# A graph network on one core: one tile of every second block taken from a table in SBUF instead of gathered

## The chip, the core and the metric

The kernel runs on one core of a Trainium2 chip. The metric is the device time of one execution in microseconds: the median of ten runs of the kernel before is 3889.19 us (3887.39 to 3890.49). The engines are TensorE (PE), VectorE (DVE), ScalarE (ACT), GpSimd (POOL) and SyncE (SP). Here GpSimd does little but issue gathers (indirect DMAs), and SyncE issues nearly all other DMAs.

## The reference

A graph of 6250 nodes with 128 features and 200,000 edges, sorted by their target node, goes through two layers. Both start from h = relu(layernorm(x)) and add their result to x. Cut to what matters:

```python
# layer 0, graph attention: 8 heads of 16
z  = h @ W;  el, er = <z, attn_l>, <z, attn_r>          # per node and head
e  = leaky_relu(el[src] + er[dst], 0.2)
a  = exp(e - segment_max(e, dst)[dst])
x += segment_sum(z[src] * a, dst) / segment_sum(a, dst) + bias
# layer 1, tensor product: s, v = parts of h, times W_up
w0..w3 = silu(silu(edge_attr_8 @ A1 + b1) @ A2 + b2) @ A3
mji = (s[src], v[src]) combined with edge_attr_4 and w0..w3   # 256 per edge
x += (segment_sum(mji, dst) / 10) @ W_out
```

Each layer so needs, for every edge, the row of a node table at src: 136 floats (z and el) in layer 0, 128 in layer 1.

## The kernel before

The edges are cut into tiles of 128, and 16 tiles make a block: NB = 98 blocks, the last one cut in two, so NG = 99 groups. Because the edges are sorted, a block's targets lie in a window of 128 nodes, and two blocks close one tile of nodes (NX = 50 tiles).

The first stage computes the table t0 (z and el by node) and writes it to DRAM. It also keeps er of each node as three bf16 parts (er3), whose sum is nearly the fp32 value.

Layer 0 is one loop over groups, `for g in range(NG - 3)` (line 1363). A step g works on several blocks at once: the logits and maxima of block g, the weights and sums of block g - 1 (called b4), the target side of block g + 1 (n1), the 0/1 matrices of block g + 2 (n2), and, every second step, the node stage of a finished tile of nodes. All this is written out by hand, and the order binds TensorE, DVE, ACT and SyncE (`tc.manual_schedule(engines=in_order)`): each runs its instructions in the order of the text. GpSimd has only gathers. The parts that matter here:
- `take_rows(g + 3)` has GpSimd gather the rows of block g + 3, one indirect DMA per tile (`gather`, line 833). The rows go to one of five buffers (`z_pool`), beside `z_first` for block 0, so block 6 needs the buffer of block 1, which is free after `sums` of that block in step 2.
- Of every third block (`by_row`: 3, 6, ... 93) the last tile is not gathered. `rows_by_row` has SyncE fetch its 128 rows one by one, each with its own DMA (line 1078), some blocks ahead. `rows_until` says how far:

```python
while rows_until.n < (block + 3) * P / 12 and next(rows, 0) is None:
    rows_until.n += 1          # one step is four rows
```

  It stands twice at the head of each step, `rows_until(rows, g + 0.5)` and `rows_until(rows, g + 1)`, with the DMAs of the nodes between them (`node_out`, `node_rows`).
- `ends_of` compares each edge's target with the 128 nodes of the window (`one_hot`, line 1097, on DVE): s, edges by nodes. `sums` (line 1234) multiplies s with the weighted rows, fp32, two records per product.
- `turned` (lines 1151 and 1153) transposes s on TensorE, four at a time, and ACT casts the result to bf16: d, nodes by edges. `er_of` (line 1162) multiplies d with the three parts of er.
- `logits`, `maxima`, `neighbours`, `weights`, `weighted` make the softmax weights; the node stage is `node_x` to `node_out`. x of all nodes stays in SBUF (`x_all`).

The bank p_n of PSUM holds a copy of iota, the er of the block (`er_p`), and the node stage's products.

Layer 1 gathers from t1 in the same way, with `by_row` too, and adds its result to x_all. Its first 24 tiles are gathered from t1z, a copy whose last three tiles of nodes are zero, while layer 0 ends.

Of the kernel before, what the change touches and what calls it, by code (L numbers as in the profile page):

```python
# [18 lines left out]
P = 128  # L19
H = 8  # L20
# [721 lines left out]
def tile_even_edges(  # L742
# [88 lines left out]
    def gather(to, table, tiles, width, first=0):  # L831
        for k, t in enumerate(tiles, first):
            nc.gpsimd.indirect_dma_start(  # L833
                out=to[:, k, :width], out_offset=None, in_=table,
                in_offset=bass.IndirectOffsetOnAxis(ap=src_col[:, t : t + 1], axis=0))
        return to
# [128 lines left out]
def even_edges(tc, v):  # L965
# [7 lines left out]
    with ExitStack() as ctx:  # L973
        const = ctx.enter_context(tc.tile_pool(name="fconst", bufs=1))
        z_pool = ctx.enter_context(tc.tile_pool(name="fz", bufs=5))
        s_pool = ctx.enter_context(tc.tile_pool(name="fs", bufs=16))
# [18 lines left out]
        x_all = const.tile([P, NX, P], F32, name="fx_all")  # L995
# [8 lines left out]
        a3p = const.tile([P, 2, P], F32, name="fa3p")  # L1004
        nc.sync.dma_start(a3p, v["a3p"])
# [4 lines left out]
        wout = const.tile([P, 2, P], F32, name="fwout")  # L1010
        nc.sync.dma_start(wout, v["wout"])
        dloc = const.tile([P, NB * KB], F32, name="fdloc")
        identb = l0c.tile([P, P], BF, name="fidentb")
        nc.vector.tensor_copy(identb, ident)
# [8 lines left out]
        with tc.tile_pool(name="fbuild", bufs=1) as build:  # L1023
            d_c = build.tile([P, TU], I32, name="fd_c")
            nc.sync.dma_start(d_c, dstc)
            d_i = build.tile([P, TG, P], I32, name="fd_i")
            nc.sync.dma_start(d_i, tiles_of(dstt, P))
            q_i = build.tile([P, TG, P], I32, name="fq_i")
            nc.sync.dma_start(q_i, tiles_of(dstt, P - 1))
            nxt_i = build.tile([P, TG], I32, name="fnxt")  # L1030
            nc.sync.dma_start(nxt_i, tiles_of(dstt, 2 * P)[:, :, 0])
            off = build.tile([P, TU], F32, name="foffs")
            nc.sync.dma_start(off, nums[:, :TU])
            nc.vector.tensor_sub(dloc[:, :TU], d_c, off)


            eq = build.tile([P, TG, MC], F32, name="feq")
            nc.vector.tensor_tensor(eq[:, :, :P], d_i, q_i, OP.is_equal)
            nc.vector.memset(eq[:, :, 0:1], 0.0)
            nc.vector.memset(eq[:, :, P : P + 1], 0.0)  # L1040
            nc.vector.tensor_tensor(eq[:, :, P + 1 : 2 * P + 1], d_i,
                                    nxt_i.unsqueeze(2).to_broadcast([P, TG, P]), OP.is_equal)
            nc.vector.tensor_tensor(eq[:, :, 2 * P + 1 :], d_i,
                                    q_i[:, :, 0:1].to_broadcast([P, TG, P]), OP.is_equal)
            for g in range(TG):
                nc.scalar.activation(masks[:, g, :], eq[:, g, :], AF.Copy, bias=-BIG, scale=BIG)

            zeros = build.tile([P, NL, P], F32, name="fzeros")
            nc.vector.memset(zeros, 0.0)
            nc.sync.dma_start(t1z[LATE * P - W0 :].rearrange("(j p) f -> p j f", p=P), zeros)  # L1050
# [5 lines left out]
        with tc.tile_pool(name="fat_ps", bufs=1, space=PSUM) as at_ps:  # L1056
            col = l0c.tile([P, P], F32, name="fcol")
            n = NB - 1
            nc.vector.tensor_copy(col[:, :n], v["src_col"][:, KB - 1 : n * KB : KB])
            p_c = at_ps.tile([P, P], F32, name="p_c")  # L1060
            nc.tensor.transpose(p_c[:n], col[:, :n], ident)
            for i, w in enumerate((ZW, P)):
                nc.vector.tensor_scalar(at[i][:n], p_c[:n], float(4 * w), None, op0=OP.mult)
# [53 lines left out]

        in_order = {mybir.EngineType.PE, mybir.EngineType.DVE, mybir.EngineType.Activation,
                    mybir.EngineType.SP}
        with tc.manual_schedule(engines=in_order), \  # L1120
                tc.tile_pool(name="l0", bufs=2) as l0, \
                tc.tile_pool(name="l0n", bufs=2) as l0n, \
                tc.tile_pool(name="l0_ps", bufs=1, space=PSUM) as l0_ps:
# [3 lines left out]
            p_n = l0_ps.tile([P, 512], F32, name="p_n")  # L1127
            er_p, iota_p = p_n[:, P : 2 * P].rearrange("p (t h) -> p t h", h=H), p_n[:, 3 * P :]
            nc.scalar.copy(iota_p, iota)

# [14 lines left out]

            def turned(c, q):
                if 4 * q < c["kt"]:
                    m = min(4, c["kt"] - 4 * q)
                    p_d = l0_ps.tile([P, 4, P], F32, name="p_d", bufs=2)
                    for k in range(m):  # L1150
                        nc.tensor.transpose(p_d[:, k, :], c["s"][q][:, k, :], ident)  # L1151
                    d = c["d", q] = l0.tile([P, 4, P], BF, name="d", bufs=4)
                    nc.scalar.copy(d[:, :m], p_d[:, :m])  # L1153
# [17 lines left out]
            def logits(c, bank="pe"):  # L1171
                kt = c["kt"]
                kr = kt * H
                e_s = l0.tile([P, KB, H], F32, name="e_s")
                pe = c["pe"] = p_n if bank == "p_n" else l0_ps.tile([P, 512], F32, name=bank, bufs=2)
                nc.vector.tensor_add(e_s[:, :kt], c["z"][:, :kt, F:], c["er"][:, :kt])  # L1176
                nc.vector.scalar_tensor_tensor(e_s[:, :kt], e_s[:, :kt], 0.2, e_s[:, :kt],  # L1177
                                               op0=OP.mult, op1=OP.max)
                nc.tensor.transpose(pe[:kr, :P], e_s[:, :kt].rearrange("p t h -> p (t h)"), ident)  # L1179
# [57 lines left out]

            def node_rows(i, n):
                nc.sync.dma_start(x_all[:, i : i + n, :],
                                  xp[i * P : (i + n) * P].rearrange("(j p) f -> p j f", p=P))  # L1240

            def with_bias(i, n):
                x_i = x_all[:, i : i + n, :]
                nc.vector.tensor_add(x_i, x_i, bias_b[:, None, :].to_broadcast([P, n, F]))

            def node_x(u):
                i, n, agg = u["i"], u["n"], u["agg"]
                x_i = x_all[:, i : i + n, :]
                if n == 1:
                    with_bias(i, n)  # L1250
                rd = l0n.tile([P, 2, H], F32, name="rd")[:, :n]
                nc.vector.tensor_scalar(rd, agg[:, :n, F:ZW], 1e-9, None, op0=OP.max)
                nc.vector.reciprocal(rd, rd)
                sums_ = agg[:, :n, :F]
                heads = sums_.rearrange("p j (h d) -> p j h d", d=D)
                nc.vector.tensor_mul(heads, heads, rd.unsqueeze(3).to_broadcast([P, n, H, D]))
                nc.vector.tensor_add(x_i, x_i, sums_)
                u["mv"] = moments(l0n, x_i, n, f"n{n}")
# [4 lines left out]
            def node_h(u):  # L1263
                i, n = u["i"], u["n"]
                rs, mr = normal(l0n, u["mv"], u["rs"], n, f"n{n}")
                xn = u["xn"] = l0n.tile([P, 2, P], F32, name="xn")
                nc.scalar.activation(xn[:, 0, :], x_all[:, i, :], AF.Identity, bias=mr[:, 0, :],
                                     scale=rs[:, 0, :])
                if n == 2:
                    nc.vector.tensor_scalar(xn[:, 1, :], x_all[:, i + 1, :], u["mv"][:, 1, 0:1],  # L1270
                                            rs[:, 1, :], op0=OP.subtract, op1=OP.mult)

            def node_t(u):
                n = u["n"]
                u["p_n"] = p_n.rearrange("p (j f) -> p j f", f=P)
                for j in range(n):
                    nc.tensor.transpose(u["p_n"][:, j, :], u["xn"][:, j, :], ident)
                h_t = u["h_t"] = l0n.tile([P, 2, P], F32, name="h_t")
                nc.scalar.activation(h_t[:, :n], u["p_n"][:, :n], AF.Relu)
# [11 lines left out]
            def node_out(u):  # L1291
                i, n, sv = u["i"], u["n"], u["sv"]
                first = i * P - W0
                for table in (t1, t1z) if i < LATE else (t1,):
                    if i == 0:
                        nc.sync.dma_start(table[: P - W0, :], sv[W0:, 0, :])
                    else:
                        nc.sync.dma_start(
                            table[first : first + n * P].rearrange("(j p) f -> p j f", p=P), sv)

# [12 lines left out]
            def take_rows(g):  # L1313
                if 0 < g < NG:
                    c = cs[g]
                    t = c["b"] * KB + c["o"]
                    c["z"] = gathered(t0, range(t, t + c["kt"] - (c["b"] in by_row)), ZW)
# [28 lines left out]
            for g in range(1, 3):  # L1346
                take_rows(g)
            masks_of(cs[0])
# [14 lines left out]
            for g in range(NG - 3):  # L1363
# [12 lines left out]
                logits(c)  # L1376
                ends_of(n2, 0)
# [3 lines left out]
                maxima(c)  # L1381
                ends_of(n2, 1)
# [5 lines left out]
                er_of(n1, 0)  # L1388
                if b4:
                    weights(b4)  # L1390
                for n in nodes:
# [3 lines left out]
                if b4:  # L1395
                    bank_of(b4)
                    weighted(b4, 0)
                turned(n1, 3)
                er_of(n1, 2)
                if b4:  # L1400
                    weighted(b4, 8)
                for n in nodes:
# [4 lines left out]
                if b4:  # L1407
                    sums(b4, 0)
                for n in nodes:
# [7 lines left out]
                if b4:  # L1417
                    sums(b4, 8)
                if g == NG - 4:
# [68 lines left out]
        with tc.manual_schedule(engines=in_order), \  # L1488
                tc.tile_pool(name="l1", bufs=3) as l1, \
                tc.tile_pool(name="l1n", bufs=2) as l1n, \  # L1490
                tc.tile_pool(name="l1_ps", bufs=2, space=PSUM) as l1_ps:

# [79 lines left out]

            def node1(i, agg):
                x_i = x_all[:, i, :]
# [10 lines left out]
            def node_out1(i):  # L1585
                x_i = x_all[:, i, :]
                if i == 0:
                    nc.sync.dma_start(out[: P - W0, :], x_all[W0:, 0, :])
# [54 lines left out]
            rows, rows_until.n, late = rows_by_row(1, t1, P), 0, []  # L1643
# [13 lines left out]
            for i, u in enumerate(us):  # L1657
                b, k0, m = u["b"], u["k0"], u["m"]
                if k0 == 0:
                    take_rows(b + 2)  # L1660
                    filled(1, b, blk[b]["z"], P)
                    edge_rows(b + 2)
                if k0 == 4:
# [43 lines left out]
            x_i = x_all[:, NX - 2 :, :]  # L1707
# [140 lines left out]
```

## Time and profile before

| | |
|---|---|
| median of ten runs | 3889.19 us |
| the profiled execution | 3889.12 us, its span 3887.3 us |
| mean granted clock of TensorE | 0.802 |
| busy in the span: PE, DVE, ACT, POOL | 73%, 57%, 36%, 75% |
| gathers, all but 32 in one group | 3024, mean 945 ns |
| rows fetched singly by SyncE | 2 x 3968 |
| layer 0, 165 to 1955 us: granted clock | 0.64 |
| layer 1, 2000 to 3867 us: granted clock | 0.97 |

The profile is of one execution. "Busy" counts the time of an engine's instructions, without waits and without the issue of DMAs, so SyncE has no busy share; its instructions are read from the timeline. A group of instructions is shown as line, engine, operation, written tile <- read tiles, count, then busy time, mean ns of one, and the idle time of the engine just before them with what ended it. Times in the timeline are microseconds from the start of the span.

### The profile page before, as it was taken

The numbers are of one execution on the slowest core, as the hardware profiler recorded it, in microseconds if no ns is written. First come the engines' busy times: TensorE is split into PE (matmuls) and PEld (weight loads), VectorE is DVE, ScalarE is ACT, GpSimd is POOL, SyncE is SP. The second block draws the span as 40 slices with busy tenths as digits, with TensorE's granted clock in tenths as the row PEclk, the third lists the DMA queues.
The fourth block names the chain that finished last, engine by engine and source line by source line (L and its number), as shares of the span: only waits on it lengthen the run. The fifth ranks groups of instructions, "written<-read, shape, count | busy, mean of one in ns | idle before, by whom it ended". The sixth has DMA issues, their size and how long they took to land. (4 is left out here: it accounts for less than half of the span.)

```text
span 3887.3 us, 62701 instructions
## 1 busy us (share of the span) xinstructions
PE 2852.6 (73%) x14785; PEld 2405.2 (62%) x14785; DVE 2225.6 (57%) x5408; ACT 1396.7 (36%) x3612; POOL 2912.7 (75%) x3096
## 2 busy tenths in 40 slices
PE   3766666666666666666678888888888777778877
PEld 3656656656666556666666666666766566656665
DVE  5544444444444444444457777677766666666666
ACT  3323232323222323232324444444444444444443
POOL 6777777777777777777777777777777777777776
PEclk6666666666666666666679999999999999999999
DMA  6222222222222222222222222222222222222222
GB/s 180 59 64 64 62 64 64 64 62 64 62 64 62 64 62 64 62 63 62 62 60 61 61 61 62 62 62 62 62 61 61 63 62 61 62 61 63 61 61 50
DMA packets 195262, 252.65 MB, mean 65 GB/s; under 512 B 78656, under 2 KB 145088, under 8 KB 194880
## 3 DMA queue, kind: packets, MB, share of 16 engines
q0 software_dynamic: 98048, 207.27, 22.5%
q1 hardware_dynamic: 96544, 41.19, 4.0%
q8 instruction: 120, 1.97, 0.2%
q14 instruction: 262, 2.15, 0.2%
q10 hardware_dynamic: 288, 0.07, 0.0%
HBM read 234.73 MB, written 13.25 MB: 64 GB/s over the span
## 5 line engine op out<-in xcount | busy, mean ns | idle before, releaser
L833 POOL DMA_INDIRECT g<-ft,fsrc x3024 | 2856.4, 945 | 922.3 <-issue 854.6
L1570 PE MATMUL p_u<-mj,s 128*128 128x256 f32 x3126 | 791.0, 397 | 211.5 <-DVE mj L1562 209.8
L1570 PEld LDWEIGHTS p_u<-mj,s 128*128 128x128 f32 x3126 | 589.3, 196 | 378.3 <-DVE mj L1562 302.9
L1234 PE MATMUL p_u<-g,s 128*128 128x136 f32 x3062 | 597.6, 376 | 0.4 <-DVE g L1229 0.4
L1234 PEld LDWEIGHTS p_u<-g,s 128*128 128x128 f32 x3062 | 571.8, 279 | 0.5 <-DVE g L1229 0.4
L1537 ACT ACTIVATE p_w<-p_w,yb 128x64 f32<-128x64 f32 x1563 | 450.7, 288 | 122.2 <-PE p_w L1533 76.4
L1553 DVE TENSOR_TENSOR vy<-g,p_i 128x384 f32<-128x384 f32 x387 | 213.4, 552 | 355.7 <-DMA g<-ft,fsrc 245.3
L1533 PE MATMUL p_w<-fa3p,h 128*128 128x256 f32 x1564 | 412.7, 387 | 0.0
L1151 PE MATMUL p_d<-fident,s 128*128 128x128 f32 x1563 | 384.9, 412 | 0.0
L1533 PEld LDWEIGHTS p_w<-fa3p,h 128*128 128x128 f32 x1564 | 290.2, 196 | 118.7 <-issue 53.1
L1176 DVE TENSOR_TENSOR e_s<-g,p_n 128x128 f32<-128x128 f32 x96 | 27.5, 287 | 578.8 <-DMA g<-ft,fsrc 558.0
L1518 ACT ACTIVATE h<-p_h,fb 128x512 f32<-128x512 f32 x196 | 134.7, 687 | 576.9 <-PE p_h L1516 576.9
L1151 PEld LDWEIGHTS p_d<-fident,s 128*128 128x128 f32 x1563 | 313.1, 226 | 37.3 <-issue 26.0
L1144 ACT COPY mk<-p_m 128x385 f32<-128x385 f32 (+1 forms) x99 | 47.6, 481 | 782.5 <-PE p_m L1141 782.5
L1229 DVE TENSOR_TENSOR g<-g,pe 128x1024 f32<-128x1024 f32 x193 | 225.6, 1209 | 129.1 <-ACT g L1220 121.1
L1153 ACT CAST d<-p_d 128x512 bf16<-128x512 f32 x391 | 228.5, 585 | 192.2 <-PE p_d L1151 141.2
L1179 PE MATMUL pe<-fident,e_s 128*128 128x128 f32 x98 | 39.3, 401 | 326.6 <-DVE e_s L1177 326.6
L1097 DVE TENSOR_TENSOR s<-p_i,fdloc 128x512 f32<-128x512 f32 x391 | 268.7, 687 | 3.8 <-ACT p_i L1512 3.8
L1097 DVE TENSOR_TENSOR s<-p_n,fdloc 128x512 f32<-128x512 f32 x391 | 266.4, 683 | 6.0 <-ACT sv L1289 2.8
L1516 PE MATMUL p_h<-ft,fa1p 128*128 128x128 f32 x1568 | 217.9, 284 | 65.9 <-DMA ft<-in_e_f_dram 65.8
L1516 PEld LDWEIGHTS p_h<-ft,fa1p 128*128 128x128 f32 x1568 | 211.4, 198 | 86.5 <-issue 67.3
L1523 ACT ACTIVATE h<-p_h,fb 128x512 f32<-128x512 f32 x196 | 134.7, 687 | 306.5 <-PE p_h L1520 306.5
(202 smaller groups left out, 3355.4 us busy)
## 6 DMA issues: line engine op xcount, KB each, us to landing
r<-ft SPq DMA_DIRECT2D x3968, 0.5 KB
r<-ft SPq DMA_DIRECT2D x3968, 0.5 KB
g<-ft,fsrc POOLq DMA_INDIRECT x3024
ft<-in_e_f_dram SPq DMA_DIRECT2D x98, 64.0 KB
yb<-in_e_y_dram SPq DMA_DIRECT2D x98, 32.0 KB
fx_all<-in_e_xp_dram SPq DMA_DIRECT2D x48, 64.0 KB
out_dram<-fx_all SPq DMA_DIRECT2D x47, 64.0 KB
ft<-sv SPq DMA_DIRECT2D x46, 64.0 KB
```

What stands on the lines that cost most here:

```text
L833: nc.gpsimd.indirect_dma_start(out=to[:, k, :width], out_offset=None, in_=table, in_offset=bass.IndirectOffsetOnAxis(ap=src_col[:, t : t + ...
L1097: nc.vector.tensor_tensor(s[:, :m], iota[:, None, :].to_broadcast([P, m, P]), dloc[:, t : t + m].unsqueeze(2).to_broadcast([P, m, P]), OP. ...
L1151: nc.tensor.transpose(p_d[:, k, :], c["s"][q][:, k, :], ident)
L1153: nc.scalar.copy(d[:, :m], p_d[:, :m])
L1229: nc.vector.tensor_mul(zh, zh, p_a[:, k0 : k0 + m].unsqueeze(3).to_broadcast([P, m, H, D]))
L1234: nc.tensor.matmul(c["p_u"][:, :ZW], c["s"][k // 4][:, k % 4, :], c["z"][:, k, :], start=c["o"] + k == 0, stop=c["o"] + k == KT[c["b"]] - 1)
L1516: nc.tensor.matmul(p_h[:, q, :], a1p[:, q0 + q, :], c["ft"], start=True, stop=True)
L1518: nc.scalar.activation(c["h1"], p_h, AF.Silu, bias=b1)
L1533: nc.tensor.matmul(w[:, k : k + n].rearrange("p k a u -> p (k a u)"), c["h2"][q // 4][:, q % 4, :], a3p[:, :n].rearrange("p k f -> p (k f) ...
L1537: nc.scalar.activation(w[:, k, ::2, :], w[:, k, ::2, :], AF.Copy, scale=c["yb"][:, k0 + k, 0:1])
L1553: nc.vector.tensor_mul(vy, v_n, y_p)
L1570: nc.tensor.matmul(blk[b]["p_u"][:, :MW], u["s"][:, k, :], u["mj"][:, k, :], start=k0 + k == 0, stop=k0 + k == KT[b] - 1)
```

## The change

In layer 0, of every second block (`dense`: 7, 9, ... 93, 44 blocks) the tile before the last (`KD` = 14) is not gathered any more. Instead:
- t0 is read back into SBUF in layer 0's first four steps (`split`), two tiles of 128 nodes at a time, and cut into three bf16 parts: `t0s`.
- `spread` has TensorE lay out the tile's sources along the free axis, the same in each partition; `ends_to` has DVE compare them with the nodes of each of NR = 17 tiles: 0/1 matrices, nodes by edges, kept in the space of `z_first`.
- `rows_of` multiplies each of the 17 with three table tiles at once (i, i + 17, i + 34: up to 408 columns), for the three parts, 51 products into one bank. Each edge so gets three candidate rows, and `taken` picks the right one on DVE with the 0/1 weights `part`.

The 0/1 matrix d is not transposed any more: the targets (`d_b`) are written to DRAM at the start (`ends`), SyncE loads those of a block into all partitions (`ends_row`, one 512 KB load per block), and DVE compares them with the node number. x is no longer kept in SBUF: layer 0 loads it by tile, as before, stores it to DRAM (`x1`), and layer 1 loads it again. iota, er and the new columns move to a bank of their own (`held`), the node stage gets p_n for itself. The order of the steps around this stays. The diff, cut to its core:

```diff
+            d_b = build.tile([P, TG, P], BF, name="fd_b")
+            off_t = build.tile([P, TG], F32, name="foff_t")
+            nc.sync.dma_start(off_t, nums[:, NB * KB : NB * KB + TG])
+            nc.vector.tensor_sub(d_b, d_i, off_t.unsqueeze(2).to_broadcast([P, TG, P]))
+            nc.sync.dma_start(ends.rearrange("g t e -> t g e"), d_b)
...
+            def split(i, n):
+                zr = l0.tile([P, 2, ZW], F32, name="zr")[:, :n]
...
+                    nc.sync.dma_start(zr, rest.rearrange("(j p) f -> p j f", p=P))
+                r = l0.tile([P, 2, ZW], F32, name="zr2", bufs=1)[:, :n]
+                nc.scalar.copy(t0s[:, 0, i : i + n, :], zr)
+                nc.vector.tensor_sub(r, zr, t0s[:, 0, i : i + n, :])
+                nc.scalar.copy(t0s[:, 1, i : i + n, :], r)
+                nc.vector.tensor_sub(t0s[:, 2, i : i + n, :], r, t0s[:, 1, i : i + n, :])
+            def spread(c):
+                nc.tensor.matmul(at_p, key[:, b : b + 1].to_broadcast([P, P]), ident, ...)
+            def ends_to(c, h):
+                n = half if h == 0 else NR - half
...
+                nc.vector.tensor_tensor(
+                    oh[:, :n], at_p.unsqueeze(1).to_broadcast([P, n, P]),
+                    place[:, h * half : h * half + n].unsqueeze(2).to_broadcast([P, n, P]), OP.is_equal)
+            def rows_of(c, k0, n):
...
+                    for s in range(3):
+                        nc.tensor.matmul(c["p_x"][:, :m, :], c["oh", k // half][:, k % half, :],
+                                         t0s[:, s, i::NR, :], start=k == 0 and s == 0, ...)
+            def taken(c):
+                nc.vector.tensor_scalar(z, c["p_x"][:, 0, :], part[:, b, 0:1], None, op0=OP.mult)
+                for r in (1, 2):
+                    nc.vector.scalar_tensor_tensor(z, c["p_x"][:, r, :], part[:, b, r : r + 1], z, ...)
+            def ends_row(b):
+                    to = ends_row.tiles[b] = l0.tile([P, KB, P], BF, name="er_d", bufs=2)
+                    nc.sync.dma_start(to, ends[g : g + 1, j * KB : (j + 1) * KB, :].to_broadcast([P, KB, P]))
             def turned(c, q):
-                    for k in range(m):
-                        nc.tensor.transpose(p_d[:, k, :], c["s"][q][:, k, :], ident)
-                    nc.scalar.copy(d[:, :m], p_d[:, :m])
+                    nc.vector.tensor_tensor(d[:, :m], ends_row.tiles[c["b"]][:, k0 : k0 + m],
+                                            node_p.unsqueeze(2).to_broadcast([P, m, P]), OP.is_equal)
...
+                nc.sync.dma_start(x1[i : i + n].rearrange("j p f -> p j f"), x_of.pop(i))   # node_out
...
+            for b in range(2):
+                ends_row(b)                       # ahead of the first rows
             for g in range(NG - 3):
...
                 logits(c)
+                ends_row(g + 2)
+                to, was = n2["b"] in dense, n1["b"] in dense
+                if to:
+                    spread(n2)
                 ends_of(n2, 0)
...                                               # masks_of, turned, maxima
+                if to:
+                    ends_to(n2, 0)
+                if was:
+                    rows_of(n1, half, 4)
...                                               # neighbours, turned, er_of
+                if was:
+                    rows_of(n1, half + 4, NR)
...                                               # weights, then: if was: taken(n1)
                     weighted(b4, 0)
+                if to:
+                    ends_to(n2, 1)
...                                               # turned(n1, 3), er_of, weighted(b4, 8)
+                if to:
+                    rows_of(n2, 0, 3)
...                                               # er_of, sums(b4, 0)
+                if to:
+                    rows_of(n2, 3, 3)
...                                               # nodes, er_sum, sums(b4, 8)
+                if to:
+                    rows_of(n2, 6, half - 6)
+                for i in range(g * 14, min(g * 14 + 14, NX), 2):
+                    split(i, min(2, NX - i))
```

In layer 1 x is loaded two blocks at a time by `node_rows1`, at the head of each even block, behind that block's `edge_rows`; the loads of a3p and wout move from the start of the kernel to the start of layer 1.

## The prediction

> **What bounds the kernel now.** I read the costliest groups first, then the busy times by stage.
>
> ```profile
> L833 POOL DMA_INDIRECT g<-ft,fsrc x3024 | 2856.4, 945 | 922.3 <-issue 854.6
> ```
>
> ```profile
> core 0: us, PE busy (x) PEld busy (x) DVE busy (x) ACT busy (x) POOL busy (x), PEclk, DMA share, GB/s
> ...
> 165.00:1955.00 1790.00, 1196.11 (x6997) 1096.44 (x6997) 819.15 (x1791) 540.49 (x1226) 1352.83 (x1434) 0.64 0.28 63
> ```
>
> GpSimd issues one gather of 128 rows after another, and its idle time is the 0.30 us of issue between them. In the first layer 1434 gathers take 1790 us, 1.248 us each. The timeline shows no gap from 43.5 us to 3867 us, across the change of layer too. So a gather less is 1.25 us less, as long as nothing makes GpSimd wait. The list of waits says how much slack the others have:
>
> ```profile
> DVE e_s L1176 <- DMA g<-ft,fsrc: 561.2, 90, 9.1
> ```
>
> The first DVE step of a block waits 6.2 us for its rows, so TensorE (67% busy), DVE (46%) and ACT (30%) have room. SyncE, which is in no busy column, has little. Its timeline, over one pair of blocks, and at the start:
>
> ```profile
> 1005.04 34.51 SPq L1078 DMA_DIRECT2D r<-ft  x84
> 1043.24 0.38 SPq L1298 DMA_DIRECT2D ft<-sv  x1
> 1043.68 1.15 SPq L1298 DMA_DIRECT2D ft1z<-sv  x1
> 1044.88 0.42 SPq L1239 DMA_DIRECT2D fx_all<-in_e_xp_dram  x1
> ```
>
> ```profile
> 59.11 4.90 SPq L1031 DMA_DIRECT2D fnxt<-in_e_dstt_dram  x1
> 64.05 3.48 SPq L1033 DMA_DIRECT2D foffs<-in_e_nums_dram  x1
> 67.63 0.63 SPq L1050 DMA_DIRECT2D ft1z<-fzeros  x1
> 68.31 1.80 SPq L1239 DMA_DIRECT2D fx_all<-in_e_xp_dram  x2
> 72.51 59.00 SPq L1078 DMA_DIRECT2D r<-ft  x152
> 131.56 0.37 SPq L1239 DMA_DIRECT2D fx_all<-in_e_xp_dram  x1
> ```
>
> Every row fetched singly costs SyncE 0.39 us (59.00/152). It keeps program order: step g=0 begins with 152 of them, the next 20 follow, and nothing else gets past. DVE was in step 0 at 92.7 us, SyncE left its rows of step 0 near 140 us. Before, that lag hurt nobody.
>
> **The gathers removed.** Blocks 7, 9, ... 93: 44 gathers x 1.248 = **-55 us**, if GpSimd never waits.
>
> **The start.** Two added things now stand behind those rows on SyncE: ends_row(2), which step 1 needs for turned(cs[2]), and the table's loads (split), seven pairs of tiles at the end of each of steps 0 to 2 and four in step 3. DVE and ACT are in order too, so step 1 cannot begin before the splits of step 0 end. The walk:
> - SyncE reaches its first row later. It loses two loads (a3p, wout: -0.9 us), but adds the load of off_t, waits for d_b on DVE (about 76.5 us, behind three ops of 1.9 us), writes ends in 1664 short pieces (4 to 5 us; the loads of that shape held the next issue 4.90 and 3.48 us), waits for its landing and issues two ends_row. The rows start near 87 instead of 72.5 us (bounds 80 and 92).
> - 172 rows x 0.39 us and one load: ends_row(2) at 155, first split load just behind.
> - A split: load 2.5 us to landing (the first x load: issued at 0.74, used at 3.28), with two buffers; ACT and DVE alternate, 2 x 0.39 (288 columns, L922) + 2 x 0.44 us (256 columns cost 0.42). So about 1.75 us each, 12.3 us for seven: step 0 ends at 170.
> - Each further step, SyncE: 40 to 44 rows (16 to 17 us), ends_row, splits. Splits of step 1 end at 199, of step 2 at 226.5, of step 3 at 250.
> - GpSimd has five buffers; block 6 needs the one of block 1, freed by the sums in step 2, some 13 us after that step starts: 212. GpSimd would have come there at 165 (79 gathers after 64 us). **Stall 47 us.** Block 7 waits for the sums of step 3 (242.5, against 230.7): **12**. Block 8 for step 4 (264 against 261): **2.5**. Step 5 then waits for ends_row(6), at 268.5: **1 to 2** more, as later in step 7.
> Sum **+63 us**; with all uncertain pieces short, 46 (rows from 72.5 us); with splits of 2.2 us and a late start, 75.
>
> **TensorE, per pair of blocks.** Removed: 32 transposes (4 take 0.60 us at the full clock, 1.07 at half): -4.8 to -8.6 us; with them go the 8 casts on ACT (585 ns, -4.7 us) and the shared bank p_n, in which er_sum waited 92 us in all for h_t and L1284 82 us for DVE. Added: 51 products of 408 bf16 columns and one fp32 product. No such stream is in the trace; the nearest rows are bf16 too: 385 columns 470 ns, 24 columns 190 ns, so 0.78 ns a column, 316 ns each, 16.1 us at the granted 0.64. What the clock does shows in the sums:
>
> ```profile
> 1903.03 3.83 PE L1234 MATMUL p_u<-g,s 128*128 128x136 f32 x16
> ...
> 1940.18 2.02 PE L1234 MATMUL p_u<-g,s 128*128 128x136 f32 x16
> ```
>
> 239 ns a record against 126, for the same products. Scaled by 0.64, a new product is 0.20 us at full and 0.40 at half clock, 10 to 21 us per pair. Net +6 at full, +13 at half clock; I take +6, because the new products fill idle time next to the sums, where the second row above ran at full. The Trainium skill ("TensorE: Matmul & The Clock Gate", Part 1) says that the clock halves after an idle window of about 3.4 us and returns after a busy one; by its 1.2 and 2.4 GHz I estimate 17.3 or 8.7 us for the 51, below these bounds.
>
> **DVE, per pair.** Eight comparisons for turned (512 columns, 683 ns as L1097; they wait for the ends_row tile, loaded two steps ahead): 5.5; ends_to, 1152 and 1024 columns (1024 cost 1.21 us): 2.55; taken, three of 136: 0.9. Plus 8.9 on some 17.9 (46% of 39.1) of a pair of 37.9. Spread writes the bank that all these read, so in that step DVE's comparisons wait for TensorE to come to it, about 1 us. Walked back to back, with full-clock rows, from the moment TensorE is free:
> - Step before a dense block's turn (g even): e_s, masks 0.5; 12 products 2.4; eight shift products 1.1; so the weights start on DVE at 4, the exponential with its table load (1.28 + 0.31) ends near 6.6, transposed and copied 7.5. DVE then has the two multiplications (1.21 each) with turned between them, to 10.9; the sums, 32 x 0.126, end at 14.5. The other 12 products lie in the gap before 7.
> - The next step (g odd): DVE waits for e_s and spread to 15.3, then has 16 us of work, 12.0 of it up to the last turned (27.3). After that TensorE has er 0.3, eight sums 2.0, 9 products 1.8, node products 1.2, eight sums 2.0, 9 products 1.8: end at 36.4 (the first 9 products lie before).
> So 36 us, up to 39.5 with most sums at half clock. GpSimd's new pair is 91 gathers per 6 blocks x 1.248 / 3 = 37.9 us (now 39.1). It is hidden, narrowly: 0, or up to 1.6 x 44 = 70.
>
> **SyncE, per 6 blocks.** Busy now: 256 rows in 100.6 us, three groups of node transfers (1.4 each), register loads 2.2: 107 of 117.4. Added: 6 ends_row (512 KB, 128 pieces of 4 KB; fa1p of that size issued in 0.43) and 3 stores of x: 9 x 0.47 = 4.2, so 111.2 of 113.7. Hidden by 2.5 us. If an ends_row holds the queue 1 us longer, as ft1z does at times (1.15 above), it is 117.2 and SyncE sets the pace: 3.5 x 15 = +52.
>
> **GpSimd's own speed.** While DVE ran long comparisons of two SBUF operands, gathers slowed:
>
> ```profile
> 70.31 1.75 POOL L833 DMA_INDIRECT g<-ft,fsrc  x1 [0.30 <-issue]
> 71.16 1.89 DVE L1041 TENSOR_TENSOR feq<-fd_i,fnxt 128x1664 f32<-128x1664 int32 x1
> ```
>
> The comparisons of L1097, with one operand in PSUM, leave them at 0.94. All the added steady work has an operand in PSUM, so 0; only d_b and split don't, and split runs while GpSimd waits: +1. The Trainium skill ("GPSIMD Engine Reference", section 8, Key points) names this contention for DVE work in a two-port mode or with two SBUF inputs; if turned counted as such, gathers would lose 0.4 to 0.8 us per comparison, which would cost over 100 us.
>
> **x in DRAM, second layer.** 49 loads of 0.47 us on SyncE, which there has 10 us per 6 blocks free; x is fetched two blocks ahead. 0. At the change of layer the last t1 rows are issued at 1984.7 and first gathered at 1989.8; the last five blocks have no dense tile, so the tail stays as it is. 0.
>
> **Sum.** The profiled execution took 3889.1 us (span 3887.3), the median of the runs is 3889.2. 3889 - 55 + 63 + 1 = **3898 us**: the start gives back what the layer saves.
>
> **Rivals.**
> - A, the likeliest (0.58): GpSimd sets the pace except at the start. 3881 to 3910.
> - B, slower (0.27): after the start SyncE or the in-order chain of TensorE and DVE needs more than 37.9 us per pair. Decides from 0.8 us more of SyncE per pair, or a half clock in most sums. 3910 to 3965. For it: both margins are under 2 us, and after the stall no buffer is in reserve. Against: TensorE packs better when it never waits (from 113 to 147 us a pair took 34 us at clock 0.70).
> - C, faster (0.12): the start costs little, because SyncE's loads are not behind the rows as I read it, or the loads land sooner; then 3834 to 3880. Against: in the timeline the 152 rows do stand ahead of L1239, as in the text.
> - D (0.03): a broadcast load cut into 2048 short pieces, or slowed gathers: above 3990.
>
> **Numbers.** This kernel's measurement can tell about 0.2%, 7.8 us. Faster than 3881: C and the edge of A, 0.13. Within: the lower half of A, 0.33. Slower: the rest, 0.54. Range 3876 to 3950.
>
> **What would show it.** GpSimd idle 40 to 75 us in total between 160 and 270 us, released by the sums L1234, and idle only by issue after; the splits as stalls of DVE on a load up to about 250 us; SyncE's first split load near 155 us; in the dense stretch 1.25 us per gather and a granted clock above 0.64. Wrong if GpSimd has no gap there (C), or waits for sums throughout the layer (B).

## The result and the profile after

The median is 3950.32 us (3944.61 to 3953.86) against 3889.18 us for the kernel before: a ratio of 1.0157, 95% interval 1.0148 to 1.0166. Forecast were 3898 us, at most 3950. The profiled execution took 3953.72 us, 3.4 more than the median; its span is 3951.8 us, 64.5 us more than before, with 44 gathers less. Where the time lies is read from GpSimd, as in the prediction. First the group of the gathers in the page (line, engine, operation, count, busy time, mean ns, idle time before):

```profile
L834 POOL DMA_INDIRECT g<-ft,fsrc x2980 | 2818.0, 946 | 1021.3 <-issue 897.0
```

A gather still takes 946 ns, but the idle time before gathers has grown from 922 to 1021 us. Worked out from the starts of the gathers, the idle time beyond the 0.30 us of issue is 70.5 us before 330 us, 38.1 us in 33 small gaps between 330 and 1980 us, and 8.4 us around the change of layer; before, there was none. 70.5 + 38.1 + 8.4 - 55 = 62: the difference of the spans, but for 2.5 us. (Before 330 us some gathers take 1.05 us or more; they cost 3.2 us more than before.) The three largest gaps of the start and the two at the change of layer, in GpSimd's timeline (start, duration, then in brackets the idle time before and its releaser):

```profile
216.58 0.94 POOL L834 DMA_INDIRECT g<-ft,fsrc  x1 [50.74 <-PE p_u L1333]
...
247.87 0.94 POOL L834 DMA_INDIRECT g<-ft,fsrc  x1 [12.09 <-PE p_u L1333]
...
274.38 0.94 POOL L834 DMA_INDIRECT g<-ft,fsrc  x1 [7.53 <-PE p_m L1232]
...
2019.62 0.94 POOL L834 DMA_INDIRECT fz_first<-ft1z,fsrc  x1 [4.60 <-DMA fx<-x]
...
2053.81 0.94 POOL L834 DMA_INDIRECT g<-ft,fsrc  x1 [4.20 <-issue]
```

The stall of the start stands where it was walked to: 47 us up to 212 was forecast, and 50.4 up to 216.6 came; then 12 up to 242.5 was forecast, and 11.8 up to 247.9 came. SyncE's timeline shows the cause that the walk named, rows first, then ends_row(2), then the splits:

```profile
88.58 58.62 SPq L1082 DMA_DIRECT2D r<-ft  x152
147.25 0.37 SPq L1341 DMA_DIRECT2D x<-in_e_xp_dram  x1
147.73 8.60 SPq L1082 DMA_DIRECT2D r<-ft  x20
156.43 0.36 SPq L1242 DMA_DIRECT2D er_d<-fends_d  x1
...
157.78 11.61 SPq L1177 DMA_DIRECT2D zr<-ft  x6
```

The gaps of the steady part were not forecast. The same stretch of layer 0, of before and then of after (the columns are PE, PEld, DVE, ACT and POOL with counts, then the granted clock, DMA share and GB/s):

```profile
330.00:1955.00 1625.00, 1087.10 (x6351) 996.37 (x6350) 741.19 (x1617) 490.13 (x1110) 1228.15 (x1302) 0.64 0.28 63
```

```profile
330.00:1955.00 1625.00, 1055.02 (x7308) 813.75 (x7308) 1091.30 (x2184) 311.04 (x784) 1199.57 (x1271) 0.80 0.36 91
```

In these 1625 us GpSimd issues 31 gathers fewer than before, so it no longer sets the pace throughout. In the list of waits (total us, times, longest) DVE now waits for the loaded targets, and SyncE's single rows wait for the same loads:

```profile
DVE d L1251 <- DMA er_d<-fends_d: 278.8, 73, 6.5
```

```profile
SPq L1082 <- DMA er_d<-fends_d: 72.2, 57, 1.9
```

The second line is the one to understand: why should the fetch of a row, into another tile, wait for an ends_row load? In the trace, the DMAs of SyncE and ScalarE carry eight semaphores in turn, and each issue waits on its own, that is for the landing of the DMA eight before it (called the ring of eight below). Two stretches of SyncE show it:

```profile
1027.22 0.35 SPq L1242 DMA_DIRECT2D er_d<-fends_d  x1
1027.67 9.98 SPq L1082 DMA_DIRECT2D r<-ft  x20
...
1039.64 6.42 SPq L1082 DMA_DIRECT2D r<-ft  x20
```

```profile
348.62 0.35 SPq L1242 DMA_DIRECT2D er_d<-fends_d  x1
351.25 8.75 SPq L1082 DMA_DIRECT2D r<-ft  x26
```

Twenty rows take 6.42 us, but 9.98 behind an ends_row: 2.2 us of that is a register load (SyncE loads the offsets of the next 32 rows ahead of every 32), and most of the rest, 1.1 us, is one held issue. Where the register load (348.97 to 351.25) comes first, the load of 512 KB has landed by the time the eighth issue is due, and nothing is held: the 26 rows behind it take 0.34 us each. By chance of the counts (172, 216, 256 rows, modulo 32) that is so at every third block. The issue itself takes only 0.35 us; the Trainium skill ("Perfetto Trace Analysis", DMA Instruction — HWDGE) says that the profile's duration of such a DMA leaves out the movement of the data, and this case agrees: DVE got the load of 1027.22 at 1031.07, some 3.8 us after the issue.

How much that is in the steady part is read from SyncE's waits between 330 and 1840 us:

```profile
SPq L1082 <- DMA er_d<-fends_d: 65.2, 52, 1.8
```

All its other waits there come to 11 us. 65.2 us in 1510 are 5.0 us per 6 blocks. The two ends_row shown above are those of blocks 10 and 45: 35 blocks in 678.6 us, 116.3 us per 6 blocks, where GpSimd's 91 gathers of 1.248 us need 113.6. Without the holds SyncE would need 111.3.

### The profile page after: what moved, and what is told of

It is laid out like the page before. It is cut to its first block, busy times and chain, and to the rows that moved or that the text cites. A ratio compares the mean times of both kernels' runs of the same rounds, so it can differ in the third digit from the quotient of the medians.

```text
span 3951.8 us, 64789 instructions
## 1 busy us (share of the span) xinstructions
PE 2769.9 (70%) x15554; PEld 2171.4 (55%) x15554; DVE 2627.8 (66%) x6094; ACT 1203.8 (30%) x3272; POOL 2874.4 (73%) x3052
## 5 line engine op out<-in xcount | busy, mean ns | idle before, releaser
L1101 DVE TENSOR_TENSOR s<-p_i,fdloc 128x512 f32<-128x512 f32 x782 | 536.1, 686 | 105.7 <-PE p_i L1187 98.6
L1333 PE MATMUL p_u<-g,s 128*128 128x136 f32 x3062 | 492.3, 329 | 0.4 <-DVE g L1328 0.4
L1211 PE MATMUL p_x<-t0s,fz_first 128*128 128x408 bf16 (+1 forms) x2244 | 473.9, 365 | 0.0
L1333 PEld LDWEIGHTS p_u<-g,s 128*128 128x128 f32 x3062 | 470.3, 236 | 0.5 <-DVE g L1328 0.4
L1251 DVE TENSOR_TENSOR d<-er_d,p_i 128x512 bf16<-128x512 bf16 x391 | 264.5, 677 | 280.3 <-DMA er_d<-fends_d 278.8
L1211 PEld LDWEIGHTS <-fz_first 128*128 128x128 bf16 x2244 | 229.6, 105 | 160.1 <-issue 33.3
L1691 DVE TENSOR_REDUCE vd<-vy 128x128 f32<-128x384 f32 x391 | 229.6, 587 | 0.0
L1689 DVE TENSOR_TENSOR p_w<-g,p_w 128x128 f32<-128x128 f32 x387 | 112.6, 291 | 165.0 <-ACT p_w L1671 129.9
L1261 PEld LDWEIGHTS <-d 128*128 128x128 bf16 x1563 | 98.7, 116 | 221.7 <-DVE d L1251 217.8
L1302 PE MATMUL pe<-mx,fshift 128*128 128x1 f32 (+1 forms) x194 | 45.0, 301 | 245.0 <-ACT mx L1288 244.8
```

The source lines that it names most:

```text
L1101: nc.vector.tensor_tensor(s[:, :m], iota[:, None, :].to_broadcast([P, m, P]), dloc[:, t : t + m].unsqueeze(2).to_broadcast([P, m, P]), OP. ...
L1211: nc.tensor.matmul(c["p_x"][:, :m, :], c["oh", k // half][:, k % half, :], t0s[:, s, i::NR, :], start=k == 0 and s == 0, stop=k == NR - 1 ...
L1251: nc.vector.tensor_tensor(d[:, :m], ends_row.tiles[c["b"]][:, k0 : k0 + m], node_p.unsqueeze(2).to_broadcast([P, m, P]), OP.is_equal)
L1333: nc.tensor.matmul(c["p_u"][:, :ZW], c["s"][k // 4][:, k % 4, :], c["z"][:, k, :], start=c["o"] + k == 0, stop=c["o"] + k == KT[c["b"]] - 1)
L1691: nc.vector.tensor_reduce(vd, vy.rearrange("p t i u -> p t u i"), AX.X, OP.add)
```

## The experiments

Theory 1: SyncE's order makes both losses, at the start by the rows ahead of ends_row and the splits, later by what an ends_row load holds up. Rivals: the work of the splits itself (start), and the chain of TensorE and DVE in the order of the text (later).

**e1: rows one block ahead instead of three, in layer 0.**

```diff
-            while rows_until.n < (block + 3) * P / 12 and ...
+            while rows_until.n < (block + rows_until.a) * P / 12 and ...   # a: 1 in layer 0, 3 in layer 1
```

> In layer 0 the rows that SyncE fetches singly run one block ahead, not three; layer 1 keeps three. Step 0 then begins with 88 of them, not 172, so ends_row(2) and the split loads come 84 x 0.39 = 33 us earlier. The steady work of SyncE is the same. Theory 1 (SyncE's program order makes the stall of the start): GpSimd's gaps before 300 us fall from 70 us to 35 to 40, the 38 us of small gaps between 300 and 1960 us stay within 10 us, the time is near 3917 us (3908 to 3927). Rival (the splits' own work on ACT and DVE and their landing set the start): gaps within 8 us of 70, the time 3942 to 3955.

Measured: 3909.73 us, ratio 1.0057 (1.0040 to 1.0074). GpSimd's gaps before 330 us are 36.8 us, 33.7 less; the steady ones 28.6, and those at the change of layer 8.2. SyncE's timeline:

```profile
114.34 7.71 SPq L1082 DMA_DIRECT2D r<-ft  x24
122.14 0.36 SPq L1242 DMA_DIRECT2D er_d<-fends_d  x1
```

ends_row(2) comes 34.3 us earlier. The rows ahead are shown to be the cause of that half of the stall; what makes the other half e1 doesn't show.

**e2, e3, e4: the loads on ScalarE's queue** (ends_row; the split loads, two chunks ahead; both).

```diff
-                    nc.sync.dma_start(to, ends[g : g + 1, ...
+                    nc.scalar.dma_start(to, ends[g : g + 1, ...
```

> The 98 broadcast loads of ends_row are issued from ScalarE's queue instead of SyncE's; everything else as after the change. Theory 1 (after the start SyncE sets the pace, because the issues behind an ends_row are held): the 38 us of small gaps between 300 and 1960 us fall below 10 us; the start stays at 60 to 70 us, because the split loads of step 0 still stand behind the rows; the time is near 3917 us (3908 to 3925). Rival (the chain of TensorE and DVE in text order sets the pace): the small gaps stay at 30 to 45 us, the time is 3945 to 3960.

> The split loads of t0 are issued from ScalarE's queue, the first two of a step after its logits, each further one two chunks ahead. ends_row stays on SyncE. Theory 1: step 0 no longer ends at 170 us but before 130, but step 1 still waits for ends_row(2), issued at 156 us; so the splits of step 2 end some 14 us earlier and the gaps before 300 us fall from 70 to 50 to 58 us; the small gaps of the steady part stay; time 3932 to 3942 us. Rival (the splits' own work sets the start): gaps within 5 us of 70, time 3944 to 3955.

> Both the ends_row loads and the split loads are issued from ScalarE's queue, so nothing that TensorE, DVE or ACT wait for at the start stands behind the single rows, and SyncE loses 6 loads per 6 blocks. Theory 1: the splits of step 2 end near 165 us, GpSimd has under 10 us of gaps before 300 us and under 10 between 300 and 1960 us; the time is 3840 to 3860 us, less than before the change. Rival for the steady part (the chain of TensorE and DVE): 30 to 45 us of small gaps stay, 3875 to 3895 us. Rival for the start (the splits' own work): 40 us or more stay before 300 us.

Measured: e2 4196.33 us (1.0789, 1.0771 to 1.0807), e3 3947.32 (1.0148, 1.0132 to 1.0165), e4 4168.00 (1.0719, 1.0701 to 1.0737). All three missed what theory 1 expected, e2 and e4 far beyond the rival too; e3's time lies in the rival's range. SyncE's waits and a stretch of its timeline in e2:

```profile
SPq L1082 <- DMA er_d<-fends_d: 407.3, 76, 11.4
```

```profile
1011.91 49.59 SPq L1082 DMA_DIRECT2D r<-ft  x84
```

In the kernel before, 84 rows took 32.5 to 34.5 us. The semaphores are handed out in the order of the text, over both queues. A row whose turn comes eight after an ends_row now waits until ScalarE, in its own order, has come to issue it, and then for the landing: up to 11.4 us. In e3 the split loads do it to the rows of the start:

```profile
86.85 72.04 SPq L1082 DMA_DIRECT2D r<-ft  x152
158.95 0.38 SPq L1349 DMA_DIRECT2D x<-in_e_xp_dram  x1
159.42 8.60 SPq L1082 DMA_DIRECT2D r<-ft  x20
168.12 0.36 SPq L1250 DMA_DIRECT2D er_d<-fends_d  x1
```

152 rows in 72.0 us instead of 58.6, so ends_row(2) comes 12 us later and the gain is gone: GpSimd's gaps before 330 us are 77.7 us, more than the rival's 70. So e3 doesn't speak for the rival. In e4, where ends_row is not behind the rows either, these gaps fall to 21.1 us, which agrees with theory 1 for the start, though under 10 was expected; the steady ones are 251. "SyncE is full" alone doesn't explain these misses; the ring of eight does.

**e5: no products.** `dense` is empty, no split; compared matrices and x in DRAM stay.

> dense is empty and the table isn't split: all tiles are gathered, while the compared 0/1 matrices (ends_row, turned) and x in DRAM stay. Theory 1: GpSimd needs 117.4 us per 6 blocks again, more than SyncE's 116.3, so the small gaps between 330 and 1980 us fall below 8 us; at the start step 1 still waits for ends_row(2) behind 172 rows (156 us), so block 6's buffer comes free near 190 us instead of 165: one stall of 20 to 30 us. The time is 3912 to 3928 us: the compare part and x in DRAM cost some 30 us by themselves. Rival (only the splits delay the start): no stall above 5 us, 3888 to 3898 us.

Measured: 3917.29 us, 1.0074 (1.0057 to 1.0090), as theory 1 had it. One stall, no gap after it:

```profile
190.90 0.94 POOL L834 DMA_INDIRECT g<-ft,fsrc  x1 [27.38 <-PE pe L1294]
```

ends_row(2) was issued at 154.69 us here. The holds are there too, 72.7 us in 60 waits, but GpSimd, with all gathers, is slower than SyncE again and hides them. So without the splits the start costs 27 us; what the splits add, by their loads or their work, is the rest of the 70.

**e6: each ends_row just before a register load.** In `rows_until`, ahead of the next four rows (where no register load comes up in the step, ends_row keeps its old place):

```diff
+                if rows_until.n % 8 == 0 and rows_until.due:      # due: [g + 2], set at the head of step g
+                    rows_until.ends_row(rows_until.due.pop())
```

> Only the place of ends_row in SyncE's order changes: it is issued just before the register load (2.16 us) that SyncE makes ahead of every 32 rows, in the same step. The traces show each DMA from SyncE waiting for the landing of the one eight before it (same semaphore), so after an ends_row the eighth issue is held some 1.2 us, unless a register load stands between. Theory 1 in this form (the ring of eight): the holds go, SyncE needs 111 to 113 us per 6 blocks, the small gaps between 330 and 1980 us fall from 38 to below 12 us; at the start little changes; 3915 to 3930 us. Rival 1 (the 512 KB load takes up the queue or the DMA engines whatever follows it): small gaps stay at 30 to 40 us, 3945 to 3955 us. Rival 2 (chain of TensorE and DVE): the same as rival 1, but with gaps released by products rather than by an ends_row load.

Measured: 3902.29 us, 1.0036 (1.0023 to 1.0049), 48 us less than the change and 13 us below the range expected. The same window:

```profile
330.00:1955.00 1625.00, 1086.38 (x7533) 838.18 (x7534) 1129.01 (x2269) 323.35 (x816) 1228.24 (x1302) 0.81 0.34 93
```

1302 gathers again, as before the change: no gap at all between 330 and 1980 us, nor at the change of layer. Of SyncE's 57 waits of a row for an ends_row one of 0.3 us is left:

```profile
SPq L1082 <- DMA er_d<-fends_d: 0.3, 1, 0.3
```

The products are all there, so the chain of TensorE and DVE is not the bound: this falls for the steady part. The edit also issues ends_row earlier in its step, and that could be a rival. SyncE's own pace decides it. Two ends_row of e6, of blocks 11 and 47:

```profile
341.18 0.35 SPq L1246 DMA_DIRECT2D er_d<-fends_d  x1
...
1007.24 0.35 SPq L1246 DMA_DIRECT2D er_d<-fends_d  x1
```

36 blocks in 666.1 us are 111.0 us per 6 blocks (111.2 over blocks 10 to 82), 5.1 to 5.3 less than in the change. In both runs SyncE works through this stretch nearly without other waits (all its waits between 330 and 1840 us come to 8 us in e6), so this is its own work. What it lost is the holds, 5.0 us per 6 blocks; an earlier place in the step leaves SyncE the same instructions, so by itself it can't shorten the six blocks.

**e7: e6 and e1 together.** **e8: also the splits spread**, five in each of steps 0 to 4, between the other work; their loads ahead of the rows, three buffers, cut in place; rows no further ahead than needed in those steps.

```diff
+                for k in range(3):
+                    split_load(g, k)                # ahead of the rows of step g
...
+                split(g, 0)                         # after maxima; (g, 1) to (g, 4) later in the step
```

> The ends_row of each step just before a register load, and the single rows of layer 0 one block ahead instead of three. Theory 1: both gains add up, start 30 to 37 us, steady below 12 us, change of layer below 4 us: 3875 to 3895 us, about the time before the change. Rival (chain of TensorE and DVE sets the steady pace): 3905 to 3915 us.

> As the run before, with rows of layer 0 no further ahead than needed in steps 0 to 4 (then slowly up to one block), and the table's splits spread: five in each of steps 0 to 4, between the step's other work instead of at its end, their loads ahead of the rows in SyncE's order (three buffers, cut in place). Theory 1: steps 0 to 4 take 20 to 23 us each from 92 us, block 6's buffer is free near 155 us, so GpSimd has less than 15 us of gaps before 330 us and less than 12 after: 3845 to 3865 us, faster than before the change. Rival (chain of TensorE and DVE): 30 to 40 us of small gaps stay, 3875 to 3895 us.

Measured: e7 3870.52 us, 0.9950 (0.9933 to 0.9966); e8 3836.80 us, 0.9864 (0.9848 to 0.9881), below both kernels and below the ranges expected. In e7 33.9 us of gaps are left, all at the start, and e7 is e6 less 31.8 us: the gains add up. In e8 there is no gap from the first gather of layer 0 to the last of layer 1. Its ends_row(2), and GpSimd's waits for the sums:

```profile
91.00 0.34 SPq L1256 DMA_DIRECT2D er_d<-fends_d  x1
93.73 7.77 SPq L1082 DMA_DIRECT2D r<-ft  x24
```

```profile
POOL g L834 <- PE p_u L1348: 3.7, 12, 0.3
```

Twelve waits of 0.3 us are the issue itself. 3889.2 - 55 = 3834: the removed gathers show in full, but for 2.6 us. e8 moves the split loads, the split work and the rows at once, so it doesn't say which of them made the 33.9 us that e7 has left.

**e9: ends_row four rows after a register load** (in e6 `% 8 == 1` for `% 8 == 0`), to bring back all holds at the early place, and **e10: e8 with 11 more dense blocks.**

> As the change, but each ends_row is issued four rows after a register load, so that 28 rows follow before the next one: the opposite of the run that placed it just before the load. Theory 1 (the ring of eight): all 98 ends_row hold the eighth issue after them, not 57 as in the profile after, for 1.27 us each: 41 x 1.27 = 52 us more of SyncE in layer 0. The gaps between 330 and 1980 us grow from 38 to 75 to 100 us, the change of layer stays at 8 us or grows; time 3985 to 4015 us. Rival (the 512 KB load costs SyncE the same wherever it stands, and the gain of the other run came from issuing it earlier in the step): gaps 0 to 40 us, time 3900 to 3955 us.

> As the run with the splits spread, with 11 more dense blocks (8, 16, ... 88), so 11 gathers less: 13.7 us if GpSimd still sets the pace everywhere. SyncE has some 2 us per 6 blocks left, DVE waits 3.5 us per pair for gathered rows. Theory 1: where three dense blocks follow each other TensorE and DVE lose that slack for a step and get it back in the next ones: gaps below 10 us, time 3820 to 3835 us. Rival (TensorE and DVE are then the bound): gaps of 1 us or more in each group of eight blocks, in all over 14 us, time 3836 us or more.

Inconclusive. e9 was run four times, e10 three times, and in these runs the kernel before took 6217 to 6299 us instead of 3889, and the traces of e9 and e10 have stalls of 10 us and more on TensorE, DVE and ACT, and GpSimd waiting for DVE, ACT and TensorE in both layers. Why is not known. Layer 1, which has no ends_row, loses time there too, so the ratios (1.0118 to 1.0144 and 1.0082 to 1.0123) say nothing of the question. How the gaps grow with the number of holds, and whether TensorE and DVE have room for more products, stays open.

## Why the prediction was wrong

- **The gathers removed, -55 us**: right. e8 shows nearly all of it.
- **The start, +63 us**: right in mechanism and nearly in size, 70.5 us. Rows from 88.6 (87 forecast), ends_row(2) at 156.4 (155), splits of step 0 to 173 (170). The stall of block 8 was 7.2 us instead of 2.5.
- **SyncE per 6 blocks, 111.2 of 113.7 us, "hidden by 2.5 us"**: the step that failed. It gave an ends_row 0.47 us, little more than the issue of fa1p (0.43), a load of the same size, and put the wait of the issues behind it at nothing. These holds cost 5.0 us per 6 blocks, so SyncE needed 116.3, more than GpSimd's 113.6. The rest of the sum was right: without the holds, in e6, it is 111.0 to 111.2. The prediction had this as its rival B and its trigger, "if an ends_row holds the queue 1 us longer", priced at +52; it was two of three ends_row, 1.25 us each, and +38 in layer 0, +8.4 at the change of layer. With 7.5 us more at the start these make 54 us, and 3898 was too low by 52 (the profiled execution, from which they are read, lies 3.4 us above the median). Two rows in SyncE's waits of before show that a load can hold a later issue; the prediction draws on neither:

```profile
SPq L1025 <- DMA fa1p<-in_e_a1p_dram: 1.5, 1, 1.5
...
SPq L1078 <- DMA ft1z<-sv: 0.8, 1, 0.8
```

  L1025 is the eighth DMA after the very load of fa1p from which the 0.43 us was taken, and waits for it.
- **The change of layer, 0**: 8.4 us. It follows from the same lag: e5 and e6, in which SyncE keeps up with GpSimd, have none there.
- **TensorE, "0.20 us at full and 0.40 at half clock", +6 per pair**: near. The trace has 12 products in 2.23 us where the granted clock is 1.00, and 9 in 2.88 where it is 0.50, so 0.19 and 0.32 us each; over the steady part the granted clock rose to 0.80.

```profile
1035.96 2.23 PE L1211 MATMUL p_x<-t0s,fz_first 128*128 128x408 bf16 x12
1057.73 2.88 PE L1211 MATMUL p_x<-t0s,fz_first 128*128 128x408 bf16 x9
```

- **The walk of 36 us a pair, hidden by GpSimd's 37.9**: that it is hidden is right, as e6 shows: with the holds gone all of it fits, without a gap. The 36 us themselves were not measured.
- **GpSimd's own speed, +1**: near, some 3 (the 3.2 us above). The mean gather of layer 0 is 944 ns before and 945 after. No gather of the steady part is slowed by the comparisons of turned, which have an operand in PSUM. Where the splits run, whose subtractions read two SBUF tiles, six gathers take 1.14 to 1.19 us instead of 0.94. That agrees with the Trainium skill ("GPSIMD Engine Reference", section 8, Key points), which names contention for DVE instructions with two SBUF inputs.
- **The choice among the rivals**: A was taken at 0.58 on a margin of 2.5 us of 113.7 on SyncE, with one term known only by its issue. B, at 0.27, had the place, and with 3910 to 3965 the time; the range ended at 3950, inside B.

## What to carry to other kernels

A DMA's price on the queue need not be its issue time: look in the queue's own waits for issues that wait for the landing of an unrelated load, and count how many DMAs stand between. A large load among many small ones costs least just ahead of something slow on the same queue (here a register load of 2.2 us, e6), and moving it to another queue can be far worse if both draw on the same semaphores (e2). What is in front of a new load in program order counts at the start: order the first steps by what the compute engines need first.

## What was not expected of the hardware

- Moving 98 loads of 512 KB from SyncE's to ScalarE's queue, with nothing else changed, cost 246 us (3950 to 4196): in this program the two queues are coupled by the eight semaphores, and 84 rows took 49.6 instead of about 34 us.
- Register loads of 2.2 us (348.97 to 351.25 above), ahead of every 32 rows, are some 15% of SyncE's time in layer 0 (8 in some 114 us), and in e6 they cover a load that lands in under 4 us.
- TensorE's granted clock between 330 and 1955 us was 0.64 before, 0.67 in e5, without the products, and 0.80 with them.
